# Layer 0 of a two-layer selective-scan network: y joins the sums' PSUM bank by an identity product on TensorE, and ScalarE reads the bank back, where VectorE added the bank to y

## The chip, the cores and the metric

The kernel runs on one core of a Trainium2 chip. The metric is the device time of one execution in microseconds. The engines are named as the profile names them: PE (TensorE), DVE (VectorE), ACT (ScalarE), POOL (GpSimd) and SP (SyncE, which only issues DMAs here). All data is float32.

## The reference, cut to what matters

The network has two layers over a batch of four images of 384 channels and 32 x 32 positions. In layer 0 each image goes through a selective scan in four directions (k = 0 to 3: rows, columns, and both reversed), and the four results are summed position by position; layer 1 has a scan in one direction with 768 channels and ends in a mixture of four experts. The part that the change concerns is the sum over the directions:

```
dA = jnp.exp(dtt[..., None] * A)
h = h * dA + (dtt * ut)[..., None] * bt[:, :, None, :]
y = jnp.einsum('bkdn,bkn->bkd', h, ct)
...
ys = ys + Ds.astype(jnp.float32).reshape(K, D)[None, :, :, None] * u
y = _cross_merge(ys, H, W).reshape(B, D, H, W)
# _cross_merge: y0 + y2 (turned back) + transposed(y1 + y3 (turned back))
```

Each of the 384 channels has a state of 16 numbers, and y is the product of the state with C, summed over the 16.

## The kernel before, in words

**Passes, parts and steps.** A pass is one image, one direction (layer 0) or one half of the channels (layer 1), and one half of the positions (T = 512 of them). There are 48 passes: 32 of layer 0 and 16 of layer 1, in an order that mixes the layers: image 0 of layer 0 (8 passes: k = 1, 3, 2, 0, two halves each), image 1 with k = 1 and 3, layer 1 of image 0, image 1 with k = 2 and 0, image 2 with k = 1 and 3, layer 1 of image 1, image 2 with k = 2 and 0, image 3 (8 passes), layer 1 of images 2 and 3. A pass has 3 parts (c, 128 channels each), and a part has 4 steps (m, four of the 16 states each): 576 steps. A step works on 128 partitions x 4 groups (x) x 512 positions. In a step:

- POOL makes dt·u·B for all four groups (`times_b`, line 1481) into one of a ring of four SBUF tiles `ss`, so the product of step i waits for the sums of step i - 4.
- ACT makes exp(dt·A) per group (`decay`, line 1487) into one of four PSUM banks `das`.
- DVE runs the recurrence per group (`scan`, line 1496) and multiplies two to four of the groups by C (`times_c`, line 1528); POOL multiplies the rest (line 1544).
- PE sums over the states (`add`, line 1517): for each group a product with the 0/1 matrix `four` into 32 partitions of one PSUM bank, `acc`. A float32 product is two matmul instructions in the trace, so an `add` is eight. The four steps of a part accumulate.

**The gather.** After the fourth step of a part the bank is read out before the next part's first product may write it. In layer 0 this is `gather0` (lines 588 to 599), all of it on DVE: for k = 1, the first direction of an image, it writes y = u·dsum + acc (line 597); for k = 3, y += acc in two instructions of 256 elements, since the columns' order makes y strided over both halves (line 599, the view is made by `in_order`); for even k, y += acc in one instruction of 512 (line 593). In layer 1 the gather is line 819, also on DVE. There is one bank `acc` for all parts.

**The order of the work.** The program is written out by a planner when the kernel is built. Each engine has streams of fixed order (`main`: scans and products with C on DVE; `gathers` on DVE; `decays` on ACT; `adds` on PE; `cs` and `bs` on POOL) with planned costs, and around them "lanes" of other work, such as normalizations, projections, the layer-0 feed-forward net and the experts. `choose` picks, per engine, what goes next by planned start times. What the planner writes is the order on each engine; on the chip each engine runs its list in that order and waits where data is late. Experts (lines 1147 to 1293) have the lowest rank: they fill gaps during the scans, and what is left runs after the last scan.

Of the kernel before, what the change touches and what calls it, by code (L numbers as in the profile page):

```python
# [13 lines left out]
ALU = mybir.AluOpType  # L14
# [5 lines left out]
HP, QP = P // 2, P // 4  # L20
NB = 4
D = 384
NC = D // P
# [76 lines left out]
PE, DVE, ACT, POOL, SP = "PE", "DVE", "ACT", "POOL", "SP"  # L100
# [150 lines left out]
def layers(ctx, tc, ins, out, const):  # L251


    nc = tc.nc
    pvt, ident, mean_w = const["pv"], const["ident"], const["mean_w"]
# [12 lines left out]
    def tiles(n, shape, name, dtype=F32, pool=None):  # L268
        return [(pool or sp).tile(shape, dtype, name=f"{name}{i}") for i in range(n)]
# [11 lines left out]
    NG, NJ = 4, 4 * NC  # L281
# [4 lines left out]
    NSR = 4  # L286
    ss = tiles(NSR, [P, NG, T], "s")
# [55 lines left out]
    acc = ps_1.tile([P, T], F32, name="acc")  # L343
# [18 lines left out]
    four = wp.tile([P, QP], F32, name="four")  # L362
# [13 lines left out]
    dsum = wp.tile([P, NC], F32, name="dsum")  # L376
# [167 lines left out]
    st = {}  # L544

    def in_order(to, halves, k, h):


        if k % 2 == 0:
            return [(to, halves[h])]  # L550
        nw = T // HW
        out = []
        for x, t in enumerate(halves):
            at = to.rearrange("p (w h) -> p w h", h=HW)[:, :, x * nw : (x + 1) * nw]
            out.append((at, t.rearrange("p c (h w) -> p c w h", w=HW)[:, :, h * nw : (h + 1) * nw, :]))
        return out
# [32 lines left out]
    def gather0(b, k, h, c):  # L589

        y = st[("y", b)]
        if k % 2 == 0:
            nc.vector.tensor_tensor(y[h][:, c], y[h][:, c], acc, ALU.add)
            return
        for (new, to), (_, u) in zip(in_order(acc, y, k, h), in_order(acc, st[("u0", b)] if k == 1 else y, k, h)):
            if k == 1:
                nc.vector.scalar_tensor_tensor(to[:, c], u[:, c], dsum[:, c : c + 1], new, ALU.mult, ALU.add)
            else:
                nc.vector.tensor_tensor(to[:, c], to[:, c], new, ALU.add)

    def post0(b, h):

# [760 lines left out]
    passes = []  # L1363
    quads = []
    for layer, b, xs in order:
        if layer == 0:
            of = [(k, k, h, i == 0, k >= 2) for k in xs for i, h in enumerate((0, 1) if k < 2 else (1, 0))]
        else:
            of = [(h, g, h, h == 0, False) for h in xs for g in range(2)]
# [12 lines left out]
    def last(layer, b, h=None):  # L1382
        return max(p for p, v in enumerate(passes) if (v["layer"], v["b"]) == (layer, b) and h in (None, v["h"]))

    jobs = []
# [17 lines left out]
    for n, q in enumerate(quads):  # L1403
        p = q["p"]
        layer, b, x = q["layer"], q["b"], q["x"]
# [9 lines left out]
    def later(f, *of):  # L1415

        return lambda: f(*of)
# [15 lines left out]
    for h in range(NT):  # L1433
# [6 lines left out]
    behind = [  # L1440
        (("post", 1, b, h), [("gather", last(1, b, h))], later(post1, b, h)) for b in range(NB) for h in range(NT)
    ]
# [23 lines left out]
    N = len(steps)  # L1466

    def place(i):

        p, j = steps[i]  # L1470
        return p, j // 4, j % 4
# [4 lines left out]
    def load(p, m, of, to):  # L1476
        rows = passes[p]["q"]["rows"][of + 4 * m : of + 4 * m + 4, cols(passes[p]["h"])]
        nc.sync.dma_start(out=to[m], in_=rows.unsqueeze(0).to_broadcast([QP, 4, T]))
# [28 lines left out]
    def keep_state(i, x):  # L1507

        p, j = steps[i]
        at = last_column(i)  # L1510
        nc.scalar.copy(state[:, passes[p]["slot"], j, x : x + 1], das[x][:, at : at + 1])  # L1511

    def add(i):

        _, c, m = place(i)
        for x in range(NG):
            nc.tensor.matmul(  # L1517
                acc[x * QP : (x + 1) * QP, :], lhsT=four, rhs=ss[i % NSR][:, x, :], start=m == 0, stop=m == 3
            )

    def gather(p, c):
        v = passes[p]
        (gather1 if v["layer"] else gather0)(v["b"], v["k"], v["h"], c)
        if c == NC - 1:
            plan.end["gather", p] = plan.end["gather", p, c]
# [22 lines left out]
    STEP, C1, SPARE = 6.6, 1.29, 3.7  # L1548
    C = (0.0, 3.5, 2.42, C1, 0.0)
    share = dict.fromkeys(range(N), 3)  # L1550
    main, gathers, decays, bs, cs, bl, cl, adds = ([] for _ in range(8))

    AT = {"scan": (0.0, 1.18, 3.6, 4.78), "mult": (2.36, 2.98, 5.96, STEP)}
    for i in range(N):
        p, part, m = place(i)
        v = passes[p]
        first = v["first"]
        after = ("scan", i, NG - 1)
        ring = [("add", i - NSR)] if i >= NSR else []
        rows = ("quad", v["q"]["n"])  # L1560
        if part == 0:
            of_b = [rows] + ([("b", i - 4)] if p else [])
            of_c = [rows] + ([("part", i - 4, x) for x in range(NG)] if p else [])
            bl.append(Op(("bt", p, m), LOAD, of_b, lambda p=p, m=m: load(p, m, NS, bts)))
            cl.append(Op(("ct", p, m), LOAD, of_c, lambda p=p, m=m: load(p, m, 0, cts)))
        bs.append(Op(("b", i), 4.58, [("dtu", p, part), ("bt", p, m), *ring], lambda i=i: times_b(i)))
        for x in range(NG):
            free = [("da free", i - 1, x)] if i else []
            if i and passes[steps[i - 1][0]]["first"]:
                decays.append(Op(("state", i - 1, x), 0.22, [("scan", i - 1, x)], lambda i=i, x=x: keep_state(i - 1, x)))  # L1570
            decays.append(Op(("da", i, x), 0.69, [("dt", p, part, x // 2), *free], lambda i=i, x=x: decay(i, x)))
        for what, x in (
            ("scan", 0), ("scan", 1), ("mult", 0), ("mult", 1), ("scan", 2), ("scan", 3), ("mult", 2), ("mult", 3),
        ):
            if what == "scan":
                op = Op((what, i, x), 1.12 if first else 1.18, [("da", i, x), ("b", i)], lambda i=i, x=x: scan(i, x))
            else:
                op = Op((what, i, x), 0.62, [("ct", p, m)], lambda i=i, x=x: times_c(i, x))
            main.append(op)
        cs.append(Op(("c", i), C1, [("ct", p, m), after, ("split", i)], lambda i=i: times_c_pool(i)))  # L1580
        wait = [("gather", (i // 4 - 1) // NC, (i // 4 - 1) % NC)] if m == 0 and i else []
        adds.append(Op(("add", i), 1.0, [("part", i, x) for x in range(NG)] + wait, lambda i=i: add(i), 0.8))
        if m == 3:
            cost = 1.35 if v["layer"] == 0 and v["k"] % 2 else 0.75
            room = [] if v["layer"] else [("have", "y", v["b"])]
            gathers.append(Op(("gather", p, part), cost, [("add", i), *room], lambda p=p, c=part: gather(p, c)))

# [47 lines left out]
    def choose(plan, e, mains, side):  # L1635
        if e == POOL:
            return pool_choice(plan, mains, side)
        if e == DVE:
            for n, (t, k, op) in enumerate(mains):
                if op.key[0] == "scan" and op.key[2] == 1:  # L1640
                    i = op.key[1]
                    share[i] = split(plan, i, t + 3.6)
                    plan.streams[POOL][0][i].cost = C[share[i]]
        best = min(mains, key=lambda x: (x[0], x[1])) if mains else None
        main_of = (best[0], (best[1], best[2])) if best else None
        side_of = (side[0], side[3]) if side else None
        if side is None or main_of is None and e in (SP, PE, DVE):
            return main_of if side is None else side_of
        start, want = side[0], side[3].want
        aged = plan.now - (side[3].ready() + LAG) > age(side[3], e)  # L1650
        if e == ACT:
            head = plan.head(ACT, 0)
            if head is None:
                return side_of
            step = head.key[1] + (head.key[0] == "state")
            due = needed(plan, step, AT["scan"][head.key[2]]) - head.cost - LAG
            if best and best[0] <= start and not aged:
                return main_of
            if start + want[1] <= due or aged:
                return side_of  # L1660
            return main_of
        if e == PE:
            d, a = plan.head(DVE, 1), plan.head(PE, 0)
            behind = (d.key[1] if d else N) - (a.key[1] if a else N)
            if behind > 1 and best[0] <= start:
                return main_of
            return side_of if start <= best[0] + (0.3 if side[3].rank < LOW else -0.3) else main_of
        if e == DVE:
            return side_of if start <= best[0] + 0.1 else main_of
        return side_of if start <= best[0] else main_of  # L1670

    plan = Plan(
        {DVE: [gathers, main], ACT: [decays], POOL: [cs, bs], PE: [adds], SP: [bl, cl]}, jobs, choose
    )
    plan.run()

# [102 lines left out]
```

## Time and profile before

| | |
|---|---|
| median of 3 runs | 5481.63 us (5467.94 to 5483.64) |
| the profiled execution | 5490.2 us, its span 5488.4 us |
| busy: PE, DVE, ACT, POOL | 4243.0, 4149.6, 3234.5, 3946.7 us |
| mean granted TensorE clock | 0.827 of full |
| last gather of layer 0 (line 593) starts | 3810.8 us |
| last `add` (line 1517) starts | 4656.5 us |

The span has two regimes. Up to about 4660 us the scans run, with DVE and POOL busy most of the time; after it PE works alone on the experts of the last two images. The busy share of an engine over the whole span mixes the two and is read by stretch instead.

### The profile page before, as it was taken

To read this page: it belongs to the slowest core of one execution; us is meant where nothing else is said; L and a number is where in the kernel's file an instruction comes from. 1 tells how busy PE (TensorE), PEld (TensorE's weight loads), DVE (VectorE), ACT (ScalarE), POOL (GpSimd) and SP (SyncE) were. 2 spreads that over 40 slices of the span, in tenths; PEclk is the share of its full clock that TensorE was granted. 3 is DMA by queue.
4 is the path that set the end of the run, shared out by engine and by line. 5 is a ranking of instruction groups with operands and counts; after the bars stand their busy time and mean duration, and the time that the engine had idled before them with its cause. 6 is when DMAs were issued, how large, how long until landed. Compare 5 with 4: busy or idle time off the path is not lost. (4 is left out here: it accounts for less than half of the span.)

```text
span 5488.4 us, 48822 instructions
## 1 busy us (share of the span) xinstructions
PE 4243.0 (77%) x13780; PEld 1805.1 (33%) x13780; DVE 4149.6 (76%) x4954; ACT 3234.5 (59%) x5779; POOL 3946.7 (72%) x1829
## 2 busy tenths in 40 slices
PE   5565578876566878886877888787888877898998
PEld 1000112211112323332333322333333334676775
DVE  5999999989889999868888999989994978100000
ACT  4454567765455767656565687767775745344342
POOL 4999999888888979758888889988993876200101
PEclk7666678977676989997988878888898888999997
DMA  3345555444434545544656444554444455556554
GB/s 118 128 152 185 183 182 186 137 148 144 140 124 159 172 140 168 166 139 162 208 185 219 164 147 147 171 173 155 157 160 141 149 188 187 172 183 202 168 172 153
DMA packets 429096, 896.35 MB, mean 163 GB/s; under 512 B 74612, under 2 KB 176152, under 8 KB 410392
## 3 DMA queue, kind: packets, MB, share of 16 engines
q1 hardware_dynamic: 371608, 701.82, 39.3%
q10 hardware_dynamic: 49024, 166.22, 8.9%
q0 software_dynamic: 8192, 25.17, 1.4%
q8 instruction: 110, 1.80, 0.1%
q14 instruction: 162, 1.33, 0.1%
HBM read 718.11 MB, written 174.95 MB: 163 GB/s over the span
## 5 line engine op out<-in xcount | busy, mean ns | idle before, releaser
L1481 POOL TENSOR_TENSOR s<-dtus,bt 128x2048 f32<-128x2048 f32 x576 | 2604.2, 4529 | 258.7 <-PE acc L1517 158.7
L1487 ACT ACTIVATE da<-dts,a 128x512 f32<-128x512 f32 x2304 | 1532.4, 685 | 984.0 <-DVE s L1528 832.5
L1517 PE MATMUL acc<-s,four 128*32 128x512 f32 x4608 | 1226.7, 733 | 579.0 <-POOL s L1544 312.3
L1528 DVE TENSOR_TENSOR s<-da,ct 128x512 f32<-128x512 f32 x1582 | 1026.2, 679 | 63.9 <-ACT state L1511 63.1
L1544 POOL TENSOR_TENSOR s<-s,ct 128x512 f32<-128x512 f32 (+1 forms) x553 | 885.7, 1602 | 208.7 <-DVE s L1496 169.9
L1496 DVE TENSOR_TENSOR_SCAN da<-da,state,s 128x512 f32<-128x512 f32 x778 | 971.5, 1280 | 52.7 <-POOL s L1481 40.2
L1496 DVE TENSOR_TENSOR_SCAN da<-da,s 128x512 f32<-128x512 f32 x804 | 955.9, 1220 | 66.5 <-POOL s L1481 49.4
L1517 PEld LDWEIGHTS acc<-s,four 128*32 128x32 f32 x4608 | 174.1, 117 | 1456.9 <-POOL s L1544 588.4
L1496 DVE TENSOR_TENSOR_SCAN s<-da,state,s 128x512 f32<-128x512 f32 x374 | 467.5, 1269 | 1.2 <-ACT da L1487 1.1
L1496 DVE TENSOR_TENSOR_SCAN s<-da,s 128x512 f32<-128x512 f32 x348 | 414.3, 1206 | 2.0 <-ACT da L1487 1.8
L1231 PE MATMUL ps<-mw,tmp 128*128 128x384 f32 x1052 | 392.0, 518 | 12.3 <-DMA mw<-in_w_dram 6.1
L1211 PE MATMUL ps<-tmp,mw 128*128 128x256 f32 (+1 forms) x1728 | 385.9, 380 | 13.3 <-DVE t L682 2.6
L1211 PEld LDWEIGHTS ps<-tmp,mw 128*128 128x128 f32 x1728 | 312.8, 207 | 139.8 <-issue 37.2
L708 PE MATMUL ps<-big,w 128*128 128x512 f32 x576 | 289.4, 645 | 29.3 <-DMA w<-in_w_in_dram 20.6
L1322 POOL DMA_INDIRECT tmp<-ys,slot x46 | 44.4, 966 | 364.9 <-DMA ys<-ct 325.6
L476 PE MATMUL ps<-xd,dtw 12*128 12x512 f32 (+1 forms) x288 | 214.4, 834 | 105.6 <-DMA dtw<-in_w_dt_dram 53.2
L497 POOL TENSOR_TENSOR tmp<-tmp,big 128x256 f32<-128x256 f32 (+1 forms) x192 | 198.8, 1063 | 101.4 <-DVE tmp L491 87.6
L1231 PEld LDWEIGHTS ps<-mw,tmp 128*128 128x128 f32 x1052 | 203.7, 201 | 206.4 <-issue 72.6
L1345 DVE TENSOR_TENSOR dtus<-dtus,da 128x384 f32<-128x384 f32 x5 | 2.8, 555 | 340.5 <-PE da L1340 340.5
L1345 DVE TENSOR_TENSOR tmp<-tmp,ps 128x384 f32<-128x384 f32 x13 | 7.2, 553 | 314.4 <-issue 292.4
L748 PE MATMUL ps<-tmp,w 128*128 128x512 f32 x288 | 168.9, 733 | 42.1 <-ACT tmp L741 39.6
L418 PE MATMUL ps<-tmp,mean_w 128*128 128x512 f32 x276 | 158.0, 719 | 49.2 <-ACT tmp L414 34.5
(411 smaller groups left out, 5454.0 us busy)
## 6 DMA issues: line engine op xcount, KB each, us to landing
mw<-in_w_dram SPq DMA_DIRECT2D x414, 384.0 KB
dts<-dts ACTq DMA_DIRECT2D x288, 512.0 KB
dtus<-dts SPq DMA_DIRECT2D x144, 1024.0 KB
dts<-tmp SPq DMA_DIRECT2D x384, 192.0 KB
bt<-rows SPq DMA_DIRECT2D x192, 256.0 KB
ct<-rows SPq DMA_DIRECT2D x192, 256.0 KB
dts<-in_w_dram SPq DMA_DIRECT2D x114, 384.0 KB
ys<-t SPq DMA_DIRECT2D x32, 768.0 KB
```

Of the source, the lines that this page charges most:

```text
L476: nc.tensor.matmul(pd, lhsT=dtw[dt_rows(q), c * P : (c + 1) * P], rhs=xd[dt_rows(q), cols(h)], start=True, stop=True,)
L497: nc.gpsimd.tensor_tensor(to, by, u[:, c], ALU.mult)
L708: nc.tensor.matmul(pi, lhsT=w[:, c, :], rhs=u[:, c], start=c == 0, stop=c == NC - 1)
L748: nc.tensor.matmul(pk, lhsT=taps[tap], rhs=xt[:, tap : tap + T], start=tap == 0, stop=tap == 3)
L1211: nc.tensor.matmul(ph[:, k * width : (k + 1) * width], lhsT=w[:, c, k * P : (k + 1) * P], rhs=turned[:, c], start=c == 0, stop=c == NC - 1,)
L1231: nc.tensor.matmul(py[k][:, :D], lhsT=by_f(hids[half_], width)[:, at_ + f, k * P : (k + 1) * P], rhs=w[:, f], start=2 * q + f == 0, stop=2 ...
L1481: nc.gpsimd.tensor_tensor(ss[i % NSR], dtus[part_of(i) % 2], rep(bts[i % 4], NG), ALU.mult)
L1487: nc.scalar.activation(das[x], dts[(2 * part_of(i) + x // 2) % 3][:, x % 2, :], AF.Exp, scale=v["a"][:, g, m : m + 1])
L1496: nc.vector.tensor_tensor_scan(d if in_psum else s, d, s, 0.0 if v["first"] else state[:, v["slot"], j, x : x + 1], ALU.mult, ALU.add)
L1517: nc.tensor.matmul(acc[x * QP : (x + 1) * QP, :], lhsT=four, rhs=ss[i % NSR][:, x, :], start=m == 0, stop=m == 3)
L1528: nc.vector.tensor_tensor(ss[i % NSR][:, x, :], das[x], cts[i % 4], ALU.mult)
L1544: nc.gpsimd.tensor_tensor(s[:, m:, :], s[:, m:, :], rep(cts[i % 4], NG - m), ALU.mult)
```

## The change

For k = 1 nothing changes. For k = 0, 2 and 3 of layer 0, before the first `add` of a part, a new function `add_y` on PE multiplies y by the identity matrix into the bank `acc` (start of the accumulation), the four `add`s accumulate on top of it, and the gather is a plain copy of the bank to y by ACT. The copy is an operation in a new ACT stream, `evicts`; the product is an operation "under" in PE's stream `adds`, which waits for the earlier gathers of the same y and for the gather of the part before. The planner's choices are adapted: on ACT an eviction goes before a decay that could start at the same time and before aged side work, and on PE the head of the stream may be an "under".

```
 def gather0(b, k, h, c):
     y = st[("y", b)]
-    if k % 2 == 0:
-        nc.vector.tensor_tensor(y[h][:, c], y[h][:, c], acc, ALU.add)
+    if k != 1:
+        for new, to in in_order(acc, y, k, h):
+            nc.scalar.copy(to[:, c], new)
         return
-    for (new, to), (_, u) in zip(in_order(acc, y, k, h), in_order(acc, st[("u0", b)] if k == 1 else y, k, h)):
-        if k == 1:
-            nc.vector.scalar_tensor_tensor(to[:, c], u[:, c], dsum[:, c : c + 1], new, ALU.mult, ALU.add)
-        else:
-            nc.vector.tensor_tensor(to[:, c], to[:, c], new, ALU.add)
+    for (new, to), (_, u) in zip(in_order(acc, y, k, h), in_order(acc, st[("u0", b)], k, h)):
+        nc.vector.scalar_tensor_tensor(to[:, c], u[:, c], dsum[:, c : c + 1], new, ALU.mult, ALU.add)
...
+def add_y(p, c):
+    v = passes[p]
+    for n, (new, of) in enumerate(in_order(acc, st[("y", v["b"])], v["k"], v["h"])):
+        for x in range(NG):
+            rows = slice(x * QP, (x + 1) * QP)
+            nc.tensor.matmul(new[rows], lhsT=ident[:, rows], rhs=of[:, c], start=n == 0, stop=False)
...
 def add(i):
+    more = v["layer"] == 0 and v["k"] != 1
...
-            acc[x * QP : (x + 1) * QP, :], lhsT=four, rhs=ss[i % NSR][:, x, :], start=m == 0, stop=m == 3
+            acc[x * QP : (x + 1) * QP, :], lhsT=four, rhs=ss[i % NSR][:, x, :], start=m == 0 and not more, stop=m == 3
...
+        if more and m == 0:
+            before = [("gather", q, part) for q in range(p) if (passes[q]["layer"], passes[q]["b"]) == (0, v["b"])]
+            adds.append(
+                Op(("under", p, part), 1.1 if v["k"] % 2 else 0.6, before + wait, lambda p=p, c=part: add_y(p, c))
+            )
...
+            if more:
+                evicts.append(
+                    Op(("gather", p, part), 0.75 if v["k"] % 2 else 0.6, [("add", i)], lambda p=p, c=part: gather(p, c))
+                )
+                continue
-            cost = 1.35 if v["layer"] == 0 and v["k"] % 2 else 0.75
+            cost = 1.35 if v["layer"] == 0 else 0.75
...
-        best = min(mains, key=lambda x: (x[0], x[1])) if mains else None
+        best = min(mains, key=lambda x: (x[0], -x[1] if e == ACT else x[1])) if mains else None
...
-                return side_of
+                return side_of if best is None or start < best[0] else main_of
...
-            if best and best[0] <= start and not aged:
+            if best and best[0] <= start and (best[1] == 1 or not aged):
                 return main_of
...
-            behind = (d.key[1] if d else N) - (a.key[1] if a else N)
+            at = (4 * (NC * a.key[1] + a.key[2]) if a.key[0] == "under" else a.key[1]) if a else N
+            behind = (d.key[1] if d else N) - at
...
-        {DVE: [gathers, main], ACT: [decays], POOL: [cs, bs], PE: [adds], SP: [bl, cl]}, jobs, choose
+        {DVE: [gathers, main], ACT: [decays, evicts], POOL: [cs, bs], PE: [adds], SP: [bl, cl]}, jobs, choose
```

`more` is true for the layer-0 passes with k other than 1: 24 passes, so 72 parts: 48 with even k and 24 with k = 3.

More of the change, by code (lines that the diff above doesn't have):

```diff
@@ L1511, in keep_state @@
         nc.scalar.copy(state[:, passes[p]["slot"], j, x : x + 1], das[x][:, at : at + 1])
+    def add_y(p, c):
[4 more added lines that the diff above has]
+                nc.tensor.matmul(new[rows], lhsT=ident[:, rows], rhs=of[:, c], start=n == 0, stop=False)
     def add(i):
-        _, c, m = place(i)
+        p, c, m = place(i)
+        v = passes[p]
+        more = v["layer"] == 0 and v["k"] != 1
         for x in range(NG):
             nc.tensor.matmul(
-                acc[x * QP : (x + 1) * QP, :], lhsT=four, rhs=ss[i % NSR][:, x, :], start=m == 0, stop=m == 3
+                acc[x * QP : (x + 1) * QP, :], lhsT=four, rhs=ss[i % NSR][:, x, :], start=m == 0 and not more, stop=m == 3
             )
@@ L1550, in layers @@
     share = dict.fromkeys(range(N), 3)
-    main, gathers, decays, bs, cs, bl, cl, adds = ([] for _ in range(8))
+    main, gathers, decays, bs, cs, bl, cl, adds, evicts = ([] for _ in range(9))
     AT = {"scan": (0.0, 1.18, 3.6, 4.78), "mult": (2.36, 2.98, 5.96, STEP)}
@@ L1581, in layers @@
         wait = [("gather", (i // 4 - 1) // NC, (i // 4 - 1) % NC)] if m == 0 and i else []
+        more = v["layer"] == 0 and v["k"] != 1
+        if more and m == 0:
[3 more added lines that the diff above has]
+            )
         adds.append(Op(("add", i), 1.0, [("part", i, x) for x in range(NG)] + wait, lambda i=i: add(i), 0.8))
         if m == 3:
-            cost = 1.35 if v["layer"] == 0 and v["k"] % 2 else 0.75
+            if more:
[4 more added lines that the diff above has]
+            cost = 1.35 if v["layer"] == 0 else 0.75
             room = [] if v["layer"] else [("have", "y", v["b"])]
```

## The prediction

> **What bounds the kernel now.** I read the page's slices first, then stretches of the span, then the rows of the gathers, and last the waits around the bank. The slices:
>
> ```profile
> PE   5565578876566878886877888787888877898998
> DVE  5999999989889999868888999989994978100000
> POOL 4999999888888979758888889988993876200101
> PEclk7666678977676989997988878888898888999997
> ```
>
> A slice is 137 us. DVE and POOL carry slices 2 to 34 (the scans), PE the last six. The stretches of layer 0, the late layer-1 scans, and the end (columns: length; busy us and instructions of PE, PEld, DVE, ACT, POOL; granted clock; DMA share; GB/s):
>
> ```profile
> 200.00:800.00 600.00, 351.88 (x835) 62.60 (x836) 568.48 (x631) 314.83 (x571) 552.24 (x241) 0.69 0.51 170
> 1500.00:1880.00 380.00, 271.26 (x817) 95.47 (x816) 350.32 (x440) 218.66 (x405) 333.27 (x149) 0.75 0.47 155
> 2680.00:3097.00 417.00, 328.66 (x1286) 163.66 (x1285) 352.48 (x447) 243.57 (x464) 340.64 (x164) 0.83 0.58 191
> 3097.00:3811.00 714.00, 579.40 (x1812) 217.67 (x1813) 668.11 (x733) 516.01 (x915) 639.96 (x280) 0.84 0.49 162
> 4660.00:5488.00 828.00, 762.80 (x3181) 555.55 (x3179) 34.31 (x99) 322.72 (x548) 70.14 (x71) 0.93 0.55 176
> ```
>
> DVE is busy 95%, 92%, 85% and 94% of the four layer-0 stretches, POOL 92, 88, 82 and 90%, ACT only 52 to 72%. Cut at the gathers, the 72 parts that change last 2180 us; DVE idles 184 us in them, under 1 us in 35, and POOL idles 314 us. So DVE ends these parts, with POOL close behind.
>
> The gathers that leave DVE, and who waits on either side of them:
>
> ```profile
> L593 DVE TENSOR_TENSOR big<-big,acc 128x512 f32<-128x512 f32 x48 | 32.7, 680 | 29.1 <-PE acc L1517 28.8
> L599 DVE TENSOR_TENSOR big<-big,acc 128x256 f32<-128x256 f32 x48 | 26.8, 610 | 14.4 <-PE acc L1517 14.4
> POOL s L1481 <- PE acc L1517: 158.7, 65, 10.1
> ACT da L1487 <- DVE s L1528: 832.5, 634, 7.9
> ```
>
> The third row is the price of a late bank: POOL has waited for the sums in 65 of 576 steps. The fourth says that ACT mostly waits for DVE.
>
> **The change part by part.**
>
> *Removed from DVE.* 48 x 0.680 + 48 x 0.610 (24 parts of two) = 32.7 + 26.8 = 59.5 us of work, and 28.8 + 14.4 = 43.2 us in which DVE stood at the gather until PE had finished the fourth sum.
>
> Not all of the work counts. Between 2074 and 2240 us the k = 3 parts of image 2 run, and after them DVE waits for layer 1 of image 1 anyway (18 us at 2240 to 2293, 62 us at 2424 to 2533): that chain starts at the last gather of image 1 (1881 us) and runs over PE, ACT, POOL and DMAs. A quarter of the k = 3 saving, 6.7 us, falls into that gap. 52.8 us count. Of the 43.2 us I count half, 21: where DVE no longer stands at the gather it sometimes meets the next late thing, a product of POOL (L1481) or a decay.
>
> *POOL as second bound.* In the 35 parts without DVE idle time POOL idles 1.64 us on the mean; the relief is 0.68 us (even k) or 1.22 us (k = 3). In 11 of them POOL has under 0.7 us left. I take 10 us off.
>
> *Added to ACT.* The nearest rows, copies from PSUM:
>
> ```profile
> L665 ACT COPY tmp<-ps 128x512 f32<-128x512 f32 x96 | 55.8, 585 | 31.4 <-PE ps L663 19.2 <-POOL s L1481 3.3 <-PE ps L476 2.7
> L571 PE MATMUL ps<-big,w 128*44 128x256 f32 x192 | 43.4, 613 | 46.0 <-DMA w<-in_w_x_dram 37.2 <-DVE big L432 5.6 <-ACT state L1511 3.2
> L571 PE MATMUL ps<-big,w 128*44 128x512 f32 x96 | 30.4, 783 | 25.3 <-DMA w<-in_w_x_dram 25.1 <-ACT t L644 0.3
> ```
>
> Even k: 48 x 0.585 = 28 us. For k = 3 no row shows ACT writing the strided y; between a contiguous copy of 256 (L1183, 0.45 us) and twice that I take 0.6: 48 x 0.6 = 29 us. Together 57 us, covered by ACT's idle time: 28 to 48% of the stretches. What can hurt is not the work but the place: ACT runs in order, so an eviction that waits for the fourth sum holds the decays behind it, and a scan waits for its decay. DVE lost 43 us in the same position, and DVE frees a `da` bank two scans and one or two products (3 to 4 us) before its next scan in it, so a decay of 0.69 us can be held some 2.5 us; this is why only half of the 43 us is counted above. Without that cover the whole 43 us come back.
>
> *Added to PE: the identity product.* Even k: eight instructions of 32 columns, the form of an `add`, which takes 1.07 us when all four groups are ready:
>
> ```profile
> 3004.72 1.07 PE L1517 MATMUL acc<-s,four 128*32 128x512 f32 x8
> L1517 PE MATMUL acc<-s,four x4608: 589/617/1064, 91.8 to 4656.5; 128*32 128x512 f32 x192
> 459.71 0.68 DVE L593 TENSOR_TENSOR big<-big,acc 128x512 f32<-128x512 f32 x1
> 460.45 0.19 PEld L1517 LDWEIGHTS acc<-s,four 128*32 128x32 f32 x4 [4.00 <-DVE big L593]
> ```
>
> A single one takes 0.617 us (median) to 1.064, by the granted clock. The Trainium skill ("TensorE: Matmul & The Clock Gate", What's actually happening) says that the gate's default is half speed and that only sustained activity opens it; bursts like these would then all run at half speed, 1.07 x 1.72 = 1.84 us, 88 us for the 48. The rows show a granted clock of 0.69, 0.75, 0.83 and 0.84 in the four stretches, each with 12 of the 48, so 1.55, 1.46, 1.33 and 1.32 us: 68 us. I take 68; full speed would be 51. For k = 3 the moving side is strided: the two L571 rows show 256 strided elements at the price of 512 contiguous ones (608 to 656 ns in all 192, never slowed by the clock). Sixteen instructions, four groups at once, two rounds for each half: 4 x 0.43 (the distance of these pairs) + 0.18 = 1.9 us, between 1.1 (no penalty) and 3.6 (four strided streams hinder each other). 24 x 1.9 = 46 us. PE gets 114 us in all, on an engine busy 59 to 81% in these stretches.
>
> *The handover of the bank.* By the skill ("Perfetto Trace Analysis", Matmuls) independent groups should rotate through banks, so that one is evacuated under the next. Here one bank serves all, and the change puts a product into the handover. By the rule each handover grows by about the product, 72 times, 114 us, more than the gain. The trace speaks against that. From the end of the fourth sum to the start of the next part's first product the median is 2.5 us (even k) and 3.2 us (k = 3), largely because that part's data is not ready yet. If I put 0.3 us of wait, the copy and the product (0.3 + 0.6 + 1.3 or 0.3 + 1.1 + 1.9 us, plus 0.05) at each of the 72 fourth sums, the first product is later in 18 cases, by 0.2 us on the mean, and POOL, four steps behind in the ring, would wait longer in one, by 0.25 us. I cost the handover at nothing; the ring of four hides it, and if it were used up the 114 us would show on POOL.
>
> *Moved.* No DMA, SP or POOL instruction moves by intent. The planner makes a new order everywhere, though, and gaps like those at 2424 and 4158 us (62 and 72 us of DVE idle) can shift by some 10 us either way. That goes into the range.
>
> *Sum at the end of layer 0* (3811 us): 52.8 + 21 - 10 = 64 us earlier. Layer 1's last two images have no changed gathers, so this is carried to the end of the scans.
>
> *What the end takes back.* Experts fill gaps of the scans. The 11 blocks of image 1 took 2949 to 4599 us, 150 us each; in the end regime a block takes 32 us (table reads at 4858, 4889, 4921, 4953 us). Each us less of scans leaves 32/150 = 0.21 us of experts to the end: 13 us of 64. And the 114 us of new PE work push some expert work out of the scans. PE still idles 20 to 40% there, so I take a sixth, 19 us. Net gain: 64 - 13 - 19 = 32 us. Against the profiled execution of 5490.2 us that is 5458; this execution is 8.6 us above the median of 5481.6, from which I get 5450.
>
> **The rivals.**
>
> *Gain swallowed* (0.16). DVE has room, but POOL, or layer 1's preparation chains, set the pace, and the new order moves the gaps. For it: POOL within 2 to 4 points of DVE; the 62 and 72 us gaps are chain, not work. Against it: 35 parts with no DVE idle. The 32 us shrink to between +16 and -16 around the median: 5466 to 5498. That the change does nothing at all is excluded: 96 DVE instructions go.
>
> *PE pays in the end* (0.32), slower. The products take the gaps in which experts ran. At full speed the displaced work is 51 + 46 = 97 us if all of it ends after the scans, where PE is busy 762.80 of 828 us, so it costs its full length. Then 64 - 13 - 97 = -46: 5528. It decides from a displaced share of (64 - 13)/97 = 53%. For it: PE idles only 3 to 5 us in many 28 us parts of 1880 to 2240 us, and image 1's last block is fetched at 4599 us, just before image 2's blocks become available. Against: PE idles some 1180 us before 4660 (4660 less its 4243.0 - 762.8 us).
>
> **How the numbers follow.** Likeliest (0.52): 5450, its own range 5408 to 5465, from all 43 us regained and little displaced, to a third displaced. The range of 8 in 10 reaches from 5408 into the PE case, to 5525, leaving its far end out. A measurement can tell about 0.3%, 16 us, from no change. Faster 0.52, same 0.16, slower 0.32.
>
> **What the profile after would show.** DVE 4090 us busy, no rows L593 and L599; copies on ACT, 48 x 0.59 and 48 x 0.6 us; 768 more matmul instructions on `acc` (48 x 8 + 24 x 16), 1.1 to 1.9 us per product; layer 0 ending near 3750 us; POOL's wait on `acc` about 160 us still. I am wrong if DVE's wait for decays grows by over 40 us, if that POOL wait doubles, or if the stretch after the last scan grows by more than the scans shrink.

## The result, and the profile after

| | before | after |
|---|---|---|
| median of 13 runs | 5481.63 us | 5495.53 us |
| ratio | | 1.0028, interval 1.0019 to 1.0036: slower |
| the profiled execution, its span | 5490.2, 5488.4 us | 5500.79, 5498.8 us |
| last sum of layer 0 ends | 3810 us | 3750 us |
| last sum of all ends (end of the scans) | 4657 us | 4605 us |
| from there to the end of the span | 831 us | 893 us |
| expert matmul instructions ahead of the end of the scans, of 4992 | 2480 | 2208 |

Medians are over all runs of a kernel. Stretches, stage ends and waits are read from the one profiled execution of each kernel. Executions of one kernel differ by 11 to 39 us here, so a difference of a few us between two stage ends is no more than a hint, and the ratios decide.

An "expert matmul" here is one with the experts' weights (lines 1211 and 1231 of before). The slices of after:

```profile
PE   5555568776566888877877888887788678898998
DVE  5999999989899998749999899999886684100000
POOL 4999998888789998758889889999867584100101
PEclk7677778988677899888888799987898888999997
```

Three of the prediction's stretches, and the end (length; busy us of PE, PEld, DVE, ACT, POOL; clock; DMA share; GB/s):

```profile
200.00:800.00 600.00, 354.89 (x1052) 69.67 (x1054) 571.80 (x626) 338.62 (x618) 562.57 (x247) 0.75 0.51 171
2680.00:3097.00 417.00, 340.39 (x1344) 151.12 (x1343) 384.37 (x474) 285.02 (x535) 373.32 (x180) 0.85 0.59 196
3097.00:3811.00 714.00, 596.88 (x2082) 225.81 (x2082) 670.99 (x731) 532.61 (x960) 656.11 (x291) 0.89 0.51 166
4605.00:5498.00 893.00, 820.50 (x3488) 602.28 (x3481) 35.22 (x100) 349.79 (x603) 72.93 (x73) 0.92 0.56 180
```

DVE is at least as full as before (95, 92 and 94% of the three stretches) and gets through the same passes sooner: layer 0 is 60 us ahead at its end, the scans are 52 us ahead. Then PE works alone for 893 us in place of 831, and is busy for 820 of them. All of the gain and 10 us more are lost after the last scan, where nothing was changed.

The new rows, and the two waits that the prediction showed of before:

```profile
L594 ACT COPY big<-acc 128x512 f32<-128x512 f32 x48 | 28.1, 584 | 40.1 <-PE acc L1525 39.9
L594 ACT COPY big<-acc 128x256 f32<-128x256 f32 x48 | 25.1, 626 | 10.9 <-PE acc L1525 10.8
L1517 PE MATMUL acc<-big,ident 128*32 128x512 f32 x384 | 63.8, 744 | 41.0 <-ACT big L594 33.6 <-ACT state L1509 6.3 <-DVE big L817 0.9
L1517 PE MATMUL acc<-big,ident 128*32 128x256 f32 x384 | 62.5, 778 | 36.2 <-ACT big L594 25.1 <-ACT state L1509 9.6 <-DVE big L597 1.4
POOL s L1479 <- PE acc L1525: 159.1, 61, 15.3
ACT da L1485 <- DVE s L1536: 733.7, 570, 12.6
```

ACT now stands at the bank for 51 us (39.9 + 10.8) where DVE stood for 43. POOL's wait for the sums (159.1 us) is where it was (158.7).

### The profile page after: what moved, and what is told of

It is laid out like the page before. It is cut to its first block, busy times and chain, and to the rows that moved or that the text cites. A ratio compares the mean times of both kernels' runs of the same rounds, so it can differ in the third digit from the quotient of the medians.

```text
span 5498.8 us, 50773 instructions
## 1 busy us (share of the span) xinstructions
PE 4263.1 (78%) x14548; PEld 1824.8 (33%) x14548; DVE 4100.6 (75%) x4862; ACT 3279.2 (60%) x5883; POOL 3942.9 (72%) x1813
## 5 line engine op out<-in xcount | busy, mean ns | idle before, releaser
L1479 POOL TENSOR_TENSOR s<-dtus,bt 128x2048 f32<-128x2048 f32 x576 | 2606.6, 4533 | 255.1 <-PE acc L1525 159.1
L1525 PE MATMUL acc<-s,four 128*32 128x512 f32 x4608 | 1153.7, 706 | 562.6 <-POOL s L1552 330.6
L1320 POOL DMA_INDIRECT s<-ys,slot x20 | 19.2, 961 | 680.6 <-DMA ys<-t 324.5
L1494 DVE TENSOR_TENSOR_SCAN s<-da,s 128x512 f32<-128x512 f32 x340 | 403.0, 1199 | 6.0 <-ACT da L1485 6.0
L1209 PE MATMUL ps<-tmp,mw 128*128 128x256 f32 (+1 forms) x1548 | 358.0, 387 | 19.9 <-DVE table L1111 5.5
L1229 PE MATMUL ps<-mw,tmp 128*128 128x384 f32 x908 | 339.5, 521 | 22.4 <-DMA mw<-in_w_dram 12.9
L1209 PEld LDWEIGHTS ps<-tmp,mw 128*128 128x128 f32 x1548 | 287.0, 205 | 136.1 <-issue 39.6
L1229 PEld LDWEIGHTS ps<-mw,tmp 128*128 128x128 f32 x908 | 176.9, 202 | 195.7 <-issue 64.6
L1509 ACT COPY state<-da 128x1 f32<-128x1 f32 x812 | 126.5, 156 | 110.6 <-DVE s L1536 62.1
L1517 PE MATMUL acc<-big,ident 128*32 128x256 f32 (+1 forms) x768 | 126.3, 761 | 77.2 <-ACT big L594 58.7
```

Source lines behind the costliest of these rows:

```text
L1209: nc.tensor.matmul(ph[:, k * width : (k + 1) * width], lhsT=w[:, c, k * P : (k + 1) * P], rhs=turned[:, c], start=c == 0, stop=c == NC - 1,)
L1229: nc.tensor.matmul(py[k][:, :D], lhsT=by_f(hids[half_], width)[:, at_ + f, k * P : (k + 1) * P], rhs=w[:, f], start=2 * q + f == 0, stop=2 ...
L1479: nc.gpsimd.tensor_tensor(ss[i % NSR], dtus[part_of(i) % 2], rep(bts[i % 4], NG), ALU.mult)
L1494: nc.vector.tensor_tensor_scan(d if in_psum else s, d, s, 0.0 if v["first"] else state[:, v["slot"], j, x : x + 1], ALU.mult, ALU.add)
L1525: nc.tensor.matmul(acc[x * QP : (x + 1) * QP, :], lhsT=four, rhs=ss[i % NSR][:, x, :], start=m == 0 and not more, stop=m == 3)
```

## The experiments

The change does two things at once: it swaps operations, and it makes the planner write a new order on every engine. The runs take them apart. "Old order" is the order that the planner of before writes, "new order" that of the planner of after. Ratios are to before, on the same chip.

### Operations and order, each alone

The old order with the new operations (the gather keeps its place in the planner's VectorE stream; the product is written with the first sum):

```
 def gather0(b, k, h, c):
+    if k != 1:
+        for new, to in in_order(acc, y, k, h):
+            nc.scalar.copy(to[:, c], new)
+        return
...
 def add(i):
+    if more and m == 0:
+        add_y(p, c)
```

> The planner of before, with its costs and its order, but the operations of after: the gather that the planner places on VectorE's stream is written as ScalarE's copy, and the identity product is written directly ahead of the first sum of the part. All other instructions keep the order of before on their engines, so as many expert matmuls as before (2480 of 4992) stand ahead of the last sum on TensorE. Theory ORDER (the gain of the swap is real and the new plan gives it back by leaving 272 more expert matmuls to the end): scans end some 40 to 60 us earlier than 4657, the stretch after them stays near 830 us, total 5420 to 5445. Theory PRODUCTS (TensorE has no room for 126 us of products before the scans end): with the order fixed the products delay the sums and the experts between them, scans end no earlier than 4640, total 5470 to 5500.

Measured: 5472.8 us, ratio 0.9987 (0.9979 to 0.9995). The total lies in the range of PRODUCTS; the stretch after the scans stays as ORDER said.

The new order with the old operations:

```
-    Op(("under", p, part), ..., lambda p=p, c=part: add_y(p, c))
+    Op(("under", p, part), ..., lambda: None)
...
 def gather0(b, k, h, c):   # as before, at the place of the eviction
-            nc.scalar.copy(to[:, c], new)
+            nc.vector.tensor_tensor(y[h][:, c], y[h][:, c], acc, ALU.add)
```

> The planner of after, with its order, but the operations of before: the eviction is written as VectorE's addition to y at the place in the plan where ScalarE's copy stood, and no identity product is written. Theory ORDER: the stretch after the scans stays near 893 us as in after, the scans end near 4650, total 5530 to 5550, slower than both. Theory PRODUCTS: without products TensorE catches up, the scans end at 4610 or earlier and the total is 5440 to 5490.

Measured: 5517.2 us, ratio 1.0067 (1.0053 to 1.0081): between the two ranges, with the long end of ORDER.

The two regimes of before, of the old order with new operations, and of the new order with old operations, in this sequence:

```profile
0.00:4657.00 4657.00, 3477.16 (x10589) 1247.65 (x10589) 4114.59 (x4854) 2911.30 (x5230) 3875.64 (x1758) 0.81 0.49 161
4657.00:5488.00 831.00, 765.80 (x3195) 557.49 (x3191) 35.06 (x100) 323.20 (x549) 71.09 (x71) 0.93 0.55 176
0.00:4644.00 4644.00, 3513.29 (x11357) 1273.15 (x11357) 4062.83 (x4758) 2952.37 (x5326) 3878.07 (x1758) 0.82 0.49 161
4644.00:5476.00 832.00, 764.86 (x3194) 556.69 (x3191) 35.06 (x100) 323.21 (x549) 71.60 (x72) 0.93 0.56 176
0.00:4627.00 4627.00, 3391.55 (x10302) 1208.66 (x10302) 4117.14 (x4859) 2886.63 (x5184) 3868.19 (x1740) 0.82 0.49 159
4627.00:5525.00 898.00, 822.26 (x3480) 602.65 (x3478) 35.03 (x100) 350.13 (x603) 72.96 (x73) 0.92 0.58 179
```

| scans end, stretch after (us), ratio | old operations | new operations |
|---|---|---|
| old order | 4657, 831, 1 | 4644, 832, 0.9987 |
| new order | 4627, 898, 1.0067 | 4605, 893, 1.0028 |

Down a column only the order differs (the planner also chooses which groups POOL multiplies by C; the two orders leave 1582 and 1586 of 2304 to DVE), along a row only the operations. The swap shortens the scans by 13 or 21 us and leaves the stretch after them alone. The order shortens the scans by 30 or 39 us and lengthens the end by 67 or 61. So the products did not push the experts out: 768 more matmul instructions ran in 4644 us, 2480 expert matmuls stood ahead of the last sum as before, and the end did not grow. The loss is there without any product. How many experts are left to the end is settled when the planner writes PE's list: it is 2480 in every kernel of the old order here, and time saved or lost on the chip moved none across the last sum.

### One part of the directions, planned anew

The change for even k alone, and for k = 3 alone, each with the planner's edits restricted to match (`more = v["layer"] == 0 and v["k"] % 2 == 0`, or `== 3`).

> The change for k = 0 and 2 alone (48 parts); k = 3 stays on VectorE. By the two profiles the even passes became 88 us shorter in sum and the k = 3 passes 4 us longer. Theory ORDER: the end of layer 0 comes 50 to 90 us before 3810; how many experts are left to the end is luck of the plan, total anywhere in 5430 to 5510. Theory PRODUCTS: half of the products, so half of the 62 us that the end grew: total 5440 to 5465.

Measured: 5536.42 us, 1.0104 (1.0086 to 1.0121); scans end 4659 us, end 855 us.

> The change for k = 3 alone (24 parts); even k stays on VectorE. If the strided product costs what the relief brings (k = 3 passes: 684 us before, 688 after), layer 0 ends within 15 us of 3810. Theory PRODUCTS: the end grows by some 30 us, total 5490 to 5520. Theory ORDER: no forecast for the end, total 5450 to 5530.

Measured: 5552.18 us, 1.0123 (1.0105 to 1.0141); scans end 4685 us, end 867 us.

Both miss. Each has a part of the change and is slower than the whole of it. A new order comes with each; the same operations in the old order give 0.9980 and 1.0002 (below), so the loss goes with the order.

### What the removed work was worth

In the old order: neither copies nor products (for k other than 1 nothing is done with the sums), copies alone, products alone. These three leave sums out of y and serve only to price the parts.

```
 neither:        gather0: return for k != 1;  add: start=m == 0, no add_y
 copies only:    gather0: nc.scalar.copy;     add: start=m == 0, no add_y
 products only:  gather0: return for k != 1;  add: add_y ahead of m == 0
```

> The order of before on every engine, but for k = 0, 2 and 3 neither an addition nor a copy nor a product: the 96 VectorE instructions are simply gone and those sums are left out of y. This is the most that taking the additions off VectorE can bring in this order. The kernel with copies and products in this order was 5.5 us faster than before, its scans 12.7 us shorter. Theory BOUND (in a fixed order VectorE's 59.5 us of additions and 43.2 us of standing at the bank were mostly not on the path; POOL, the sums and the side chains set the pace): scans end 4630 to 4650, total 5455 to 5472. Theory PRICE (the relief is some 60 us as predicted, but copies and products cost most of it again): scans end near 4600, total 5410 to 5435.

> The order of before, with ScalarE's copies of the bank to y, but no identity product: y becomes the last direction's sum alone. Theory BOUND: as without both, 5455 to 5475. Theory PRICE, if ScalarE standing at the bank in place of VectorE is the price (57 us of waits there in the kernel with both): 5465 to 5475 while the kernel without both is under 5440; if the products are the price: 5415 to 5440.

> The order of before, with the identity products, but no copy of the bank: y keeps the sum of k = 1, and the other directions' sums are left out. No engine reads the bank in these 72 parts, so TensorE goes from part to part without a handover. Theory BOUND: 5455 to 5475. Theory PRICE: if the products are the price 5465 to 5480; if the copies are, under 5440.

| old order | scans end | ratio |
|---|---|---|
| additions on DVE (before) | 4657.1 | 1 |
| neither | 4617.1 | 0.9931 (0.9916 to 0.9946) |
| copies only | 4626.1 | 0.9971 (0.9961 to 0.9982) |
| products only | 4633.8 | 0.9965 (0.9953 to 0.9977) |
| both | 4644.4 | 0.9987 (0.9979 to 0.9995) |

With neither, the scans are 40 us shorter, and the median is 37 us lower (5445.5 against 5482.3 us on the same chip): that is all that taking 59.5 us of work and 43.2 us of standing off DVE brings in this order. By the ends of the scans the copies give 9 us back, the products 17, both 27. By the ratios it is 22, 19 and 31 us, each to some 10 us, so the copies may cost as much as the products. Copies alone (5464.8 us) and products alone (5464.3) fall in the range of BOUND, the kernel without either falls between the two theories: each is half right.

The scans with neither, to be set beside those of before above:

```profile
0.00:4617.00 4617.00, 3448.83 (x10589) 1246.07 (x10589) 4061.64 (x4758) 2907.06 (x5230) 3874.25 (x1758) 0.82 0.50 162
```

DVE's idle time is 542 us in before and 555 us here, though 43.2 us of it were taken away: 56 us of other waits came in their place, which is most of the 63 us that are missing. Two rows of before up to 3800 us, then the same of the kernel with neither:

```profile
DVE s L1528 <- ACT state L1511: 59.8, 19, 10.9
DVE da L1496 <- ACT da L1487: 20.0, 16, 6.0
...
DVE s L1534 <- ACT state L1507: 70.6, 28, 12.0
DVE da L1492 <- ACT da L1483: 31.2, 20, 4.4
```

DVE meets late state copies and late decays (11 us more of each) and many other small waits instead.

### Where the copies' and products' price lies

In the old order: even k alone, k = 3 alone, then both with the product moved ahead of the third step's sums, and even k so.

```
-    if more and m == 0:          # with start=n == 0 in add_y, start=m == 0 and not more in add
+    if more and m == 2:          # with start=False in add_y,  start=m == 0 in add
         add_y(p, c)
```

> The order of before; copies and products for k = 0 and 2 alone (48 parts, contiguous y), k = 3 stays on VectorE. With all three directions in this order the k = 3 passes stayed at 684 us in sum and the even passes became 22 us shorter. Theory STRIDE (the strided product, 16 instructions for a part of k = 3, eats its gain): total 5456 to 5466, some 16 to 22 us faster than before, faster than the kernel with all three (5472.8). Theory EVEN PRICE (every part gains the same little): two thirds of 5.5 us, 5474 to 5480.

> The order of before; copies and products for k = 3 alone (24 parts, strided y). Theory STRIDE: no gain or a loss, 5478 to 5496. Theory EVEN PRICE: a third of the gain, 5473 to 5480.

> The order of before with copies and products for all three directions, but the product stands ahead of the third step's sums in place of the first's, so that the next part's first sum needs only the copy of the bank. The products cost 17 us of the scans when they stand in the handover (scans end 4634.4 with products alone, 4617.1 with neither). Theory HANDOVER (they cost because the bank is handed over later): most of the 17 us goes, scans end 4626 to 4632, total 5455 to 5464. Theory PE TIME (they cost because TensorE is in order and each takes 1 to 2 us ahead of other work): as with the product first, 5469 to 5476.

> As the kernel with the product mid-part, but for k = 0 and 2 alone. Theory STRIDE with HANDOVER: the fastest so far of those that keep the sums, 5450 to 5460. STRIDE with PE TIME: as even k with the product first, 5456 to 5466. EVEN PRICE: 5470 to 5478.

| old order, new operations | product first | product mid-part |
|---|---|---|
| k = 0, 2, 3 | 0.9987 (0.9979 to 0.9995) | 0.9966 (0.9952 to 0.9980) |
| k = 0, 2 | 0.9980 (0.9968 to 0.9992) | 0.9981 (0.9973 to 0.9989) |
| k = 3 | 1.0002 (0.9992 to 1.0013) | |

k = 3 with the product in the handover gains nothing. With the product mid-part for all, the ratio is that of copies only (0.9971) within the noise, and the scans end 2 us later: no price of the products shows there, though PE does the same work. HANDOVER is the better reading in this order, but the intervals of the first row just meet, and for even k the place makes no difference: 5470.9 and 5472.5 us, the first between STRIDE and EVEN PRICE, the second in the range of EVEN PRICE. k = 3 alone lies in the range of STRIDE.

The traces show what the place does to the handover. From the end of the fourth sum to the first sum of the next part the mean over the 72 parts is 5.8 us in before, 7.1 with the product first and 5.8 with it mid-part. What the product and its weight loads waited for on PE, first in the handover, then mid-part:

```profile
  ACT state L1509: 56.3, 16
  ACT big L594: 45.1, 29
  issue: 44.2, 82
...
  issue: 75.1, 135
```

In the handover the product waits for ACT (45 us are put down to the bank's copy, 56 us to a state copy); mid-part the profile shows no wait. In the change's own order the same move brought nothing:

> The order of after, product mid-part in place of first. In the order of before this brought 12 us over the product first. If the products' price is the handover in this order too: 5478 to 5490. If ScalarE's place in the new order already hides the handover: 5490 to 5498, as after.

Measured: 5497.34 us, 1.0025 (1.0017 to 1.0033), as after. Yet the product's wait for the copy was longer in this order, and it went. One row of after, then one of this kernel:

```profile
  ACT big L594: 161.2, 78
...
  issue: 68.6, 141
```

The mean handover fell from 6.9 to 5.5 us, and the time did not follow. So a later bank does not always cost time. What it costs depends on the order; why was not looked into.

### Is the order's cost caused by the change, or would any touch do?

A planned cost of before is touched (0.70 for 0.75), then the planner's step length (6.55 and 6.7 for 6.6) in before and in after. The operations on y stay. The planner also decides from the step length how many of the 2304 groups POOL multiplies by C in place of DVE, so the last column counts those left to DVE.

```
-        cost = 1.35 if v["layer"] == 0 and v["k"] % 2 else 0.75
+        cost = 1.35 if v["layer"] == 0 and v["k"] % 2 else 0.70
...
-    STEP, C1, SPARE = 6.6, 1.29, 3.7
+    STEP, C1, SPARE = 6.55, 1.29, 3.7     # or 6.7
```

> The kernel before, with one planned cost touched: a gather of 512 elements is planned with 0.70 us in place of 0.75 (the trace has 0.68). The operations are those of before; only the order moves. In this order 2292 of the 4992 expert matmul instructions stand ahead of the last sum (before 2480, after 2208). Theory ORDER IS LUCK (the order of before is a good draw, and any touch of the plan costs about what the change's new order cost, 39 us): 5500 to 5530, the stretch after the scans 870 to 885 us. Theory ORDER IS CAUSED (the new ACT stream and the products in the plan push the experts back): 5475 to 5490, as before.

> The kernel before with one constant of the planner touched: STEP, the planned length of a step, 6.55 in place of 6.6. Operations as before, order new. 2576 expert matmul instructions ahead of the last sum (before 2480). Theory LUCK: somewhere in 5465 to 5520, and if experts ahead of the last sum are paid for by longer scans at one for one, 5475 to 5500 with scans ending later than 4670. Theory CAUSED: within 10 us of before, 5472 to 5492.

> The kernel before with STEP = 6.7. Operations as before, order new. 2124 expert matmul instructions ahead of the last sum, fewer than in after (2208). Theory LUCK: 5490 to 5530, the stretch after the scans 910 to 930 us. Theory CAUSED: the experts left over are made up by shorter scans, 5472 to 5492.

> The kernel after with STEP = 6.55. Operations as after, order new; 2208 expert matmul instructions ahead of the last sum, as in after. Theory LUCK: a scatter like that of the touched kernels before, less some 15 us for the operations. Theory CAUSED: 5490 to 5505, as after.

> The kernel after with STEP = 6.7. Operations as after, order new; 2176 expert matmul instructions ahead of the last sum. Theory LUCK: a scatter like that of the touched kernels before, less some 15 us. Theory CAUSED: 5490 to 5510.

| operations, order | ratio | scans end | stretch after | expert matmuls ahead | products with C on DVE |
|---|---|---|---|---|---|
| old, before | 1 | 4657 | 831 | 2480 | 1582 |
| old, cost 0.70 | 1.0018 (1.0008 to 1.0027) | 4607 | 880 | 2293 | 1578 |
| old, step 6.55 | 0.9968 (0.9953 to 0.9983) | 4662 | 798 | 2577 | 1560 |
| old, step 6.7 | 1.0179 (1.0154 to 1.0204) | 4641 | 928 | 2125 | 1456 |
| old, order of after | 1.0067 (1.0053 to 1.0081) | 4627 | 898 | 2208 | 1586 |
| new, after | 1.0028 (1.0019 to 1.0036) | 4605 | 893 | 2208 | 1586 |
| new, after, step 6.55 | 1.0085 (1.0058 to 1.0111) | 4642 | 896 | 2208 | 1587 |
| new, after, step 6.7 | 1.0063 (1.0042 to 1.0085) | 4604 | 917 | 2176 | 1492 |

The regimes of the cost touched (first two lines) and of step 6.55:

```profile
0.00:4607.00 4607.00, 3423.88 (x10376) 1219.64 (x10376) 4110.39 (x4845) 2895.03 (x5186) 3874.93 (x1742) 0.81 0.49 160
4607.00:5487.00 880.00, 807.93 (x3408) 591.55 (x3404) 35.80 (x105) 341.32 (x586) 72.08 (x73) 0.92 0.58 179
0.00:4662.00 4662.00, 3430.13 (x10696) 1248.09 (x10696) 4106.80 (x4832) 2921.67 (x5250) 3905.03 (x1754) 0.82 0.50 163
4662.00:5460.00 798.00, 743.81 (x3085) 540.59 (x3085) 35.24 (x100) 306.82 (x524) 62.59 (x64) 0.92 0.57 173
```

A touch of 0.05 us in one planned cost, with the operations on y as before, gives the same picture as after: scans 50 us shorter, end 49 us longer. So experts move across the last sum without any help from the change. The stretch after the scans follows the experts left over: from 2577 to 2125 instructions ahead it grows from 798 to 928 us, 0.29 us for each. What that saves in the scans differs from plan to plan (50, -5 and 16 us for the three).

What the order costs on balance is another question, and the forecasts don't settle it. The cost touched hit CAUSED with its total and LUCK with its end; step 6.55 came out below both ranges, step 6.7 above both, and the two touches of after lie above CAUSED's. Step 6.7 is no neutral touch: it gives 126 more products with C to POOL, so its +1.8% mixes the order with moved work (step 6.7 of after gives it 94). The two touches that leave the split nearly alone moved before by +0.18 and -0.32%. The order of after, at +0.67% with the old operations, lies outside that. All five plans made with the change's planner edits (three here, two with a part of the directions) are slower than before, in spite of the operations. One difference shows in DVE's waits for decays up to 3800 us, here of before, of the cost touched, of the order of after with the old operations, and of after:

```profile
DVE da L1496 <- ACT da L1487: 20.0, 16, 6.0
DVE da L1496 <- ACT da L1487: 25.9, 12, 6.3
DVE da L1496 <- ACT da L1487: 56.3, 24, 17.8
DVE da L1494 <- ACT da L1485: 73.6, 31, 16.6
```

Luck explains that experts moved to the end. That it explains the whole cost is not shown: an effect of the planner edits is not excluded, and two neutral plans are too few to tell.

### The best of both

The new operations with the product mid-part, in the order of step 6.55:

> The planner of before with STEP = 6.55 (its order was 0.32% faster with VectorE's additions), and the copies with the product mid-part (0.34% faster in the order of before). If order and operations add up, scans end near 4640, the stretch after them is near 798 us, total 5436 to 5450. If the operations' gain belongs to the order of before alone, 5455 to 5475.

Measured: 5468.02 us, 0.9971 (0.9960 to 0.9981). It beats both kernels, but the parts do not add up: that order alone gives 0.9968, the operations alone, in the order of before, 0.9966. It is the second of the two forecasts that came true. The swap's worth is -0.39% in the order of after (1.0028 against 1.0067), -0.13 to -0.34% in that of before, and nothing that shows in this one. Why it is nothing here was not looked into.

## Why the prediction was wrong, by its own steps

Forecast 5450 and faster; measured 5495.5 and slower, inside the range. Two of the three signs of error that the prediction named came: DVE's wait for decays grew by 71 us (over 40), and the end grew by 62 us while the scans shrank by 52. In the old order the swap alone gains 0.13%, 7 us, where 32 were forecast; the new order then costs more than that.

- **What the end takes back** is the step that failed. It had 32 us: 13 for shorter scans, 19 for PE's products. The profile has 62, and both reasons were wrong. Shorter scans left no experts over: with neither copies nor products the scans were 40 us shorter and the end was 834 us against 831. Products displaced none: with them in the old order the end was 832 us. It grew because the new order left 272 more expert matmul instructions to it.
- **Moved** is where that belongs. The prediction gave the new order "some 10 us either way". It is worth 23 to 39 us here. The direction of the end could have been read before any run, by counting the expert matmuls ahead of the last sum in the two programs; why the order's cost on balance is this large stays open. The rival with PE had the place right (experts left to the end) and the cause wrong.
- **The sum at the end of layer 0**, 64 us forecast, 60 measured, is right by luck. There the operations are worth 12 us (3810 to 3798, old order) or 27 (3777 to 3750, new order); the other 48 or 33 us are the order's.
- **Removed from DVE**: 52.8 + 21 us, less 10 for POOL. With nothing in its place the removal brought 40, where 64 were forecast. The busy time and the waits were read correctly; what fell short is the share that lay on the path. "Under 1 us in 35" of the 72 parts did not mean that DVE's time would come back: 56 us of other waits took the place of those removed, late decays and states among them.
- **The handover at nothing, the copies covered**: they cost 27 us together by the scans, 31 by the ratios. The replay of the 72 handovers gave 0.2 us of delay for the next part's first sum on the mean (its 18 late cases come out of the trace; the medians beside it do not, they are 4.3 and 6.1 us, not 2.5 and 3.2). The trace with the product first has 1.3 us. The replay moved one thing and held the rest.
- **Sizes**: copies 53 us (forecast 57); products 126 us busy (114): k = 3 takes 62.5/24 = 2.6 us a part, not 1.9, even k 1.3. The 0.45 us read for a contiguous copy of 256 (L1183) is too high: those of 256 take 0.37, and the strided ones 0.63. POOL's wait on `acc` stayed, as said. DVE's wait for decays grew from 27 to 98 us. Up to 3800 us, with both forms of the scan, it is 23 us in before, 67 in the order of after with the old operations and no copies, and 89 in after, so most of the growth is the order's.
- The two rules of the Trainium skill: by the one on the clock ("TensorE: Matmul & The Clock Gate", What's actually happening), that only sustained activity lifts it from half speed, the products of even k were estimated at 88 us; the rows gave 63.8, near the 68 from the granted clock. The rule on rotating banks ("Perfetto Trace Analysis", Matmuls) was set aside too lightly: its full 114 us did not come, but the handovers grew, and in the order of before the product outside the handover lost almost nothing. In the order of after taking it out brought nothing.

## What to carry to other kernels

When a planner writes the order, a change of operations is two changes; put the new operations into the old order and the old operations into the new one before saying what either is worth. Touch a constant of the plan that should mean nothing and measure that too: here it moved the time by -0.3 to +0.2%, as much as the change did. Count first that the touch left the work on each engine alone; one of the constants here did not. Where low-priority work fills the gaps of one regime and the rest runs in the next, count how much of it stands ahead of the boundary, since that count, not the length of the first regime, set the end.

## What the hardware showed beyond that

- The mean granted clock rose from 0.827 to 0.844 in after, and in the stretch 200 to 800 us from 0.69 to 0.75. In the old order, products alone have 0.74 in that stretch and neither has 0.70. But the new order with the old operations has 0.74 there too, without a product, so more matmul instructions are not the only way to a higher clock.
- A copy by ACT of 256 elements into the strided y takes 626 ns, of 512 in a row 584, of 256 in a row some 370: the stride costs a copy as much as twice the elements.
